# LSTM outer steps in a fused graph network: five nested outer products and two direct ones in place of four and three

## The chip, the cores and the metric

The kernel runs on one core of a Trainium2 chip. The number that counts is the device time of one execution in microseconds (us); lower is better. The engines that matter are TensorE (PE; its weight loads have a row of their own, PEld), VectorE (DVE), ScalarE (ACT) and GpSimd (POOL); loads and stores are issued by SyncE (SP). TensorE writes its products to PSUM, which has eight banks here, each wide enough for 512 fp32 columns. Everything is fp32.

## The reference, cut to what matters

Four layers are applied to x of shape (128, 64, 256), each as x = x + f(relu(layernorm(x))), with a 64 x 64 adjacency. Layer 0 is two graph convolutions and then LSTMs; layers 1 to 3 (a graph convolution with two batch norms, a three-part graph convolution, masked attention) are not touched by the change. The LSTM part of layer 0:

```python
def _lstm_last(Wih, Whh, bih, bhh, xs):
    N, _, Hd = xs.shape
    bias = bih + bhh
    def step(carry, x_t):
        h, c = carry
        g = x_t @ Wih.T + h @ Whh.T + bias
        i, f, gg, o = jnp.split(g, 4, axis=-1)
        c = jax.nn.sigmoid(f) * c + jax.nn.sigmoid(i) * jnp.tanh(gg)
        h = jax.nn.sigmoid(o) * jnp.tanh(c)
        return ((h, c), None)
    ...
for p in range(1, MAX_SKIP + 1):
    nw = Tv // p
    wins = h[:, :nw * p, :].reshape(Bv * nw, p, Hd)
    last = _lstm_last(Wih[p - 1], Whh[p - 1], bih[p - 1], bhh[p - 1], wins)
    idx = jnp.arange(nw) * p + (p - 1)
    h = h.at[:, idx, :].set(last.reshape(Bv, nw, Hd))
```

So for p = 1, 2, 3, 4 the 64 time positions are cut into windows of p successive ones, an LSTM runs p steps through each window from a zero state, and its last hidden state takes the place of the window's last position. The next p sees what the last one wrote. Hd is 256, so the four gates together have 1024 rows.

## The kernel before, in words

**Blocks and steps.** In the LSTM stage (about 340 to 1170 us of the profiled span) features lie across the 128 partitions in two chunks, and the columns are (window, batch) pairs. They are cut into blocks of N columns: 512 for p = 2 and p = 4, 352 and 320 for p = 3. Two blocks, n = 0 and n = 1, form a pair and are computed together; two pairs (the states s = 1, then s = 0) form a group, and the steps of the two alternate. A group begins with `first_step` for each pair (the step j = 0, with no h yet; matmuls at L875, reads of their banks at L884, L888 and L891), and goes on with one outer step per pair for each j = 1 to p - 1. p = 2 has two groups with two outer steps each, p = 3 two groups with four each, p = 4 one group with six: 18 outer steps. The last of them is called `fin`, and the next layer's work (the "seam") begins beside it.

**An outer step** (`outer_step`, L942) computes all gates of both blocks, G = x Wih + h Whh. It treats this as a 2 x 2 block product, (x or h) against the gate pairs (i, g) and (f, o) for the two column blocks, and computes it in the Strassen-Winograd way, with seven products of sums instead of eight: products 1 (x of block 0 with Wih of i, g), 2 (h of block 0 with Whh of i, g), 3, 4, 5, 6 and 7. The result has four parts, called by row and column "11" (i, g of block 0), "12" (i, g of block 1), "21" (f, o of block 0) and "22" (f, o of block 1), each an SBUF tile [128, 2 gates, 2 chunks, 512]. The sums of inputs are T1 = x1 - x0 (L1057, DVE), T2 = h1 - T1 (L1060, POOL), T3 = h1 - x1 (L1063, DVE) and T4 = h0 - T2 (L1066, POOL). The sums of weights (S1 to S4) and the inner sums of W1 and W2 are computed once in the graph stage on POOL, kept in DRAM (`summed`, `kept`), and loaded for each p.

**Two ways for one product.** Each outer product has two gates x 256 x 256 weights. A *direct* one (`direct`, L996 to L1007) is eight matmuls of N columns: four (gate, chunk) pairs k = 0 to 3 in the order `CHAIN`, with two contraction halves each. Pair k goes to the bank of that name, k0 to k3. Products 1, 6 and 7 are direct before, and 6 and 7 add into the banks that 1 began; after the second half of each product the bank is read (`chained`, L1013 to L1021): for 1 a copy by ACT into "11", for 6 a DVE add that makes "12" from "22" and the bank, for 7 two DVE adds, into "21" and "22". A *nested* product (`strassen`, L972 to L984) does the same kind of seven-product scheme once more on halves, in the order

```python
INNER = (("a", 1), ("c", 2), ("a", 6), ("b", 5), ("a", 7), ("b", 3), ("a", 4))
```

where each item is a bank and a half product. "5.b3" below is the item at position 3, counted from 0, of outer product 5, which is in bank b; so the items of a product are a0, c1, a2, b3, a4, b5 and a6 ("4.0" of a direct product is its first slot, "chained 7.2" the read of bank k2 after product 7). One item has two matmuls of N/2 columns, one for each gate. Products 5, 2, 4 and 3 are nested before. Bank a takes four of the items and adds them up one after the other, and is read after each; bank b takes two and is read after each; c takes one. There are two banks for a (a0, a1), used in turn by the products, and one each for b and c. The reads are `take` (L986 to L994): an ACT copy (L992) where a product is the first to write a part (items 0, 2, 3 and 6 of products 5 and 4), and otherwise a DVE add into the part (L994). The half products need sums of the halves of their inputs, four POOL subtractions of N/2 columns for each product (`inner_sum`, L967).

**What follows in a step.** When all products that belong to a part are in, ACT applies the gate functions (`act`, L1027), POOL multiplies i by g (`in_times_g`, L1037), the cell by f (`keep`, L1040), adds (`plus`, L1043), ACT takes tanh of the cell into the o-part's neighbour (`squash`, L1046), and DVE multiplies it by o (`out`, L1048): into h, or, in the last step of a window, into x. Much of this runs beside the next step's matmuls.

**What sets the order.** The kernel schedules by hand. One slot is one item of a nested product (two half-width matmuls) or one matmul of a direct one. `SEQ` (L936) spreads the 28 nested and 24 direct slots evenly over a step, 52 in all. Every operation is put into a list of events with a planned time in slots (`at`, `tick`; `prep` is a tick not earlier than the other operands' h), and the list is issued in order of time. So on each engine the order is fixed and each instruction waits only for its operands and buffers; planned times do nothing else. Loads are on SP's queue in the same list (`plan`, `load_r` L808, `fetch` L824, `fetch_s3`): while the last step of one p is computed, weights for the next are brought in. `places` (L777) tells where in SBUF each of these lie.

Of the kernel before, what the change touches and what calls it, by code (L numbers as in the profile page):

```python
# [14 lines left out]
P = 128  # L15
# [5 lines left out]
def kernel(ctx: ExitStack, tc: tile.TileContext, a: dict, out: bass.AP):  # L21
# [318 lines left out]
    SUMS = {"X": 1536, "W1": 1792, "W2": 1792, "S1": 1792, "S2": 1024, "S3": 1024, "S4": 1792}  # L340
# [8 lines left out]
    def staging(p):  # L349
# [21 lines left out]
        def kept(name, v):  # L371
            return lambda: nc.sync.dma_start(summed[p, name], v)

        def x_sum(k):
# [6 lines left out]
        work = [*(inner(W1, k) for k in (0, 1, 3)), *(inner(W2, k) for k in (0, 1, 3)),  # L381
                *(outer(add, S1_, OF_, W2, b) for b in (0, 2)), *(outer(sub, S2_, S1_, IG, b) for b in (0, 2)),
                inner(W2, 2), *(inner(S1_, k) for k in range(4)),
# [3 lines left out]
        stores = {9: ("S2", wbf[:, 5632:6656]), 10: ("W2", w2), 14: ("S1", wcf), 17: ("W1", w1),  # L387
# [389 lines left out]
    def places(p):  # L777
# [3 lines left out]
        def row(v, size):  # L781
            return chunks(v[:, :size]) if size > 0 else None

        a["W1"], a["W2"] = Blocks(2, wbf[:, 3584:5376]), Blocks(2, wbf[:, 5376:])
        a["T4"] = chunks(txf[:, : 2 * n])
        if p == 2:
            a["R"], a["X"] = Blocks(4, wbf[:, :2048]), Blocks(3, wbf[:, 2048:3584])
            a["S1"], a["S2"], a["S3o"] = Blocks(2, wcf), Blocks(2, thA[:, :1024]), Blocks(1, thA[:, 1024:])
            a["S4"] = Blocks(2, wbf[:, 2816:3328], th[:, :1280])
            a["T1"], a["T1s"], a["T2"] = chunks(waf[:, :1024]), sums(waf[:, 1024:1792], 3, h), chunks(waf[:, 1792:2816])  # L790
            a["s"], a["T3"] = sums(waf[:, 2816:], 3, h), chunks(txf[:, 1024:])
        elif p == 3:
            a["R"], a["X"] = Blocks(4, wcf[:, :1536], waf[:, :512]), Blocks(3, waf[:, 512:2048])
            a["S1"], a["S2"], a["S3o"] = Blocks(2, wbf[:, :1792]), Blocks(2, thA[:, :1024]), Blocks(1, thA[:, 1024:])
            a["S4"] = Blocks(2, th, wcf[:, 1536:])
            a["T1"], a["T1s"] = chunks(wbf[:, 1792:2496]), sums(wbf[:, 2496:3024], 3, h)
            a["T2"], a["s"], a["T3"] = (chunks(waf[:, 2048:2752]), sums(waf[:, 2752:3280], 3, h),
                                        chunks(txf[:, 1024:1728]))
        else:
            a["R"], a["X"] = Blocks(4, wbf[:, :2048]), Blocks(3, wbf[:, 2048:3584])  # L800
            a["S1"], a["S2"], a["S3o"] = Blocks(2, waf[:, 512:2304]), Blocks(2, wcf[:, :1024]), None
            a["S4"] = Blocks(2, wbf[:, 2048:3584], txf[:, 1792:])
            a["T1"] = chunks(waf[:, 2304:3328])
            a["T1s"] = [waf[:, 3328:], waf[:, :256], waf[:, 256:512]]
            a["T2"], a["T3"], a["s"] = chunks(th[:, :1024]), chunks(thA[:, :1024]), sums(wcf[:, 1024:], 3, h)
        return a

    def load_r(p):  # L808
        to, v = pl[p]["R"], weights_of("WihT", p)
        for h in range(2):  # L810
            for c in range(2):
                nc.sync.dma_start(to[2 * h + c][:, 0:2], v[h, c][:, 0:3:2])
                nc.sync.dma_start(to[2 * h + c][:, 2], v[h, c][:, 3])
        fetch_s3(p, 1)

# [8 lines left out]
    def fetch(p, name, lo=0, hi=7):  # L824
# [3 lines left out]
        hi = min(hi, v.shape[1])  # L828
# [4 lines left out]
    def input_sums(st, j):  # L833
# [4 lines left out]
        for k in range(len(t), 4):  # L838
            t.append(wide(tx[:, k, : st["N"]]))
# [14 lines left out]
    def wih_of(p, k, gi):  # L854
# [3 lines left out]
        if m < 4 and k != 7:  # L858
            return pl[p]["R"][m][:, g]
        return pl[p]["X"][(S1, S2, S3, S4).index(m)][:, g]  # L860
# [46 lines left out]
    def first_step(t0, st, tags, names):  # L907
# [20 lines left out]
        for n in range(2):  # L928
# [7 lines left out]
    SEQ = sorted([((i + 0.25) * 52 / 28, "S", i) for i in range(28)] +  # L936
                 [((k + 0.5) * 52 / 24, "D", k) for k in range(24)])
    AT = {(kind, i): n for n, (_, kind, i) in enumerate(SEQ)}
    CHAIN = ((0, 1), (1, 1), (0, 0), (1, 0))
    FN = {(0, 0): AF.Sigmoid, (0, 1): AF.Tanh, (1, 0): AF.Sigmoid, (1, 1): AF.Sigmoid}  # L940

    def outer_step(t0, st, j, tags, fin):  # L942

        N, p, blk, B = st["N"], st["p"], st["blk"], {}
        l, H, a, last = p - 1, N // 2, dict(pl[p]), j == p - 1
        if fin:
            v = gates[tags["spare"]].rearrange("p n c t -> p (n c t)")
            a["T3"], a["late"] = chunks(v[:, :1024]), sums(v[:, 1024:1792], 3, 256)
# [12 lines left out]

        def data(pr):
            v = a["T1"][:, :, :N] if pr == 5 else a["T4"][:, :, :N] if pr == 4 else h(pr == 3)
            b = {(c, d): v[:, c, d * H : (d + 1) * H] for c in range(KC) for d in range(2)}
            return b, [s[:, :H] for s in a["T1s" if pr == 5 else "late" if fin and pr != 2 else "s"]]

        def inner_sum(pr, k, engine=nc.gpsimd):  # L967
            b, s = data(pr)
            engine.tensor_sub(*((s[0], b[0, 1], b[0, 0]), (s[1], b[1, 1], s[0]),
                                (b[0, 1], b[1, 1], b[0, 1]), (s[2], b[1, 0], s[1]))[k])  # L970

        def strassen(pr, i):  # L972
# [7 lines left out]
            d = (b[0, 0], b[1, 0], b[1, 1], s[2], s[0], s[1], b[0, 1])[k - 1]  # L980
            w = a[{5: "S1", 2: "W1", 4: "W2", 3: "S4"}[pr]][OF[k]]
            for g in range(2):
                nc.tensor.matmul(B[pr, name][:, g * H : (g + 1) * H], w[:, g, :], d, start=(new and g == 0),  # L983
                                 stop=(name, k) in (("a", 4), ("b", 3), ("c", 2)), skip_group_check=True)  # L984

        def take(pr, i):  # L986
# [3 lines left out]
            to = tile_of({5: "22", 2: "11", 4: "21", 3: "12"}[pr])[:, :, hc, d * H : (d + 1) * H]  # L990
            if pr in (5, 4) and i in (0, 2, 3, 6):
                nc.scalar.copy(to, v)  # L992
            else:
                nc.vector.tensor_add(to, to, v)  # L994

        def direct(pr, k, c):  # L996
            hc, g = CHAIN[k]
            if pr == 1 and c == 0:
# [4 lines left out]
            else:  # L1003
                w = (a["R"] if pr == 1 else a["S2"])[m][:, g]
            d = x(0, c) if pr == 1 else a["T2" if pr == 6 else "T3"][:, c, :N]
            to = wide(B[k][:, :N]) if pr == 1 else B[k][:, :N]
            nc.tensor.matmul(to, w, d, start=(pr == 1 and c == 0), stop=(c == 1), skip_group_check=True)  # L1007
# [5 lines left out]
        def chained(pr, k):  # L1013
# [3 lines left out]
            elif pr == 6:  # L1017
                nc.vector.tensor_add(part("12", k), part("22", k), v)
            else:
                for m in ("21", "22"):  # L1020
                    nc.vector.tensor_add(part(m, k), part(m, k), v)  # L1021

        def act(m, g, hc):
# [3 lines left out]
            nc.scalar.activation(v, v, FN[r, g], bias=lbias[:, l, b : b + 1])  # L1027
# [20 lines left out]
        def out(n):  # L1048
            m = ("21", "22")[n]
            if last:  # L1050
                for c in range(KC):
                    (nc.gpsimd if fin and n else nc.vector).tensor_mul(x(n, c), wide(gate_(m, 0)[:, c]), wide(gate_(m, 1)[:, c]))
                return
            nc.vector.tensor_mul(h(n), gate_(m, 0), gate_(m, 1))
# [13 lines left out]
        one = j == 1 and st["s"] == 1  # L1068
# [5 lines left out]
        for c in range(KC):  # L1074
            tick(-26 + 0.6 * c if one else -30.5 + 1.6 * c, T1, c)
        for k, s in ((0, -23 if one else -28), (1, -22), (3, -21)):
            tick(s, inner_sum, 5, k)
        prep(-11, T2)
        prep(-10.9, inner_sum, 5, 2)
        for k, s in ((0, 1), (1, 2), (3, 3)):  # L1080
            prep(s, inner_sum, 2, k)
        late = 8 if one else 5
        prep(late, T4)
        prep(late + 0.1, inner_sum, 2, 2)
        late = 18 if fin else 7 if one else 1
        for c in range(KC):
            prep(late + 0.6 * c, T3, c)
        for k, s in ((0, 25), (1, 26), (3, 27), (2, 28)):
            prep(s, inner_sum, 4, k)
        for k, s in ((0, 38), (1, 38.5), (3, 39), (2, 39.5)):  # L1090
            prep(s, inner_sum, 3, k)

        for n, (_, kind, i) in enumerate(SEQ):
            if kind == "S":
                mi, i = divmod(i, 7)
                tick(n, strassen, (5, 2, 4, 3)[mi], i)
                tick(n + 1.1, take, (5, 2, 4, 3)[mi], i)
            else:
                di, i = divmod(i, 8)
                tick(n, direct, (1, 6, 7)[di], *divmod(i, 2))  # L1100
                if i % 2:
                    tick(n + 1.15, chained, (1, 6, 7)[di], i // 2)
        e = AT["S", 13] + 2.2
        for i, (g, hc) in enumerate(((0, 0), (1, 0), (0, 1), (1, 1))):
            tick(e + 0.9 * i, act, "11", g, hc)
        tick(e + 4, in_times_g, 0)
        for k, (hc, g) in enumerate(CHAIN):
            e = AT["D", 17 + 2 * k] + 2.6
            for n in range(2):
                tick(e + 0.9 * n, act, ("21", "22")[n], g, hc)  # L1110
        e = AT["D", 19] + 4.2
        for n in range(2):
            tick(e + 0.2 * n, keep, n)
        tick(e + 0.1, plus, 0)
        tick(54.6, squash, 0)
        for i, (g, hc) in enumerate(((0, 0), (1, 0), (0, 1), (1, 1))):
            tick((51.3, 53.5)[hc] + 0.1 * g if fin else (58.2, 61.2)[hc] + 1.2 * g, act, "12", g, hc)
        e = 56.2 if fin else 63
        halves = fin or last and st["s"] == 0
        for c in range(KC if halves else 1):  # L1120
            c = slice(c, c + 1) if halves else slice(0, KC)
            tick(e, in_times_g, 1, c)
            tick(e, plus, 1, c)
        tick(61 if fin else 58.5, out, 0)
        squashed, done = (6.5, 8.8) if last and p < NL else (5, 8) if N < 512 else (4.2, 6)
        tick(e + squashed, squash, 1)
        tick(e + done, out, 1)
        st["h_at"] = t0 + e + done
        return t0 + 52
# [4 lines left out]
    def plan(t, p, *when):  # L1134
        for s, fn, *args in when:
# [3 lines left out]
    plan(t, 2, (2, load_r), *((8 + 3 * k, fetch, name) for k, name in enumerate(("X", "W1", "W2", "S1", "S2"))),  # L1139
         (25, fetch, "S4", 2, 7), (28, fetch_s3, 0))  # L1140
    for p in range(1, NL + 1):
        pairs = pairs_of(p)
        for k in range(0, len(pairs), 2):
# [15 lines left out]
            if p == 2:  # L1159
                plan(t, p, (8, fetch, "S4", 0, 2))  # L1160
# [845 lines left out]
```

## Time and profile before

| | |
|---|---|
| median of 3 runs | 1822.1 us |
| lowest and highest | 1821.66 and 1826.21 us |
| the profiled execution's own time | 1826.36 us |
| its span | 1824.6 us |
| granted TensorE clock | 0.999 of full speed |
| PE busy in the span | 1800.3 us |
| DVE, ACT, POOL busy | 1179.4, 988.5, 1205.9 us |
| PE at L983 (nested) and L1007 (direct), share of the chain that ended last | 20% and 17% |

The rows of busy time are of one profiled execution. Matmuls overlap their neighbours, so PE's busy time can cover small gaps. A row of a group of instructions names line, engine, operation, the tile written and the tiles read, the count, busy time and mean of one, and then the idle time of the engine ahead of them with what ended it. In a timeline, the columns are the start in us from the start of the span, the duration, the engine, the line and operation, the tiles, the shape and the number of instructions joined in one row; what stands in brackets at a row's end is the engine's idle time ahead of it and what released it.

### The profile page before, as it was taken

To read this page: it belongs to the slowest core of one execution; us is meant where nothing else is said; L and a number is where in the kernel's file an instruction comes from. 1 tells how busy PE (TensorE), PEld (TensorE's weight loads), DVE (VectorE), ACT (ScalarE), POOL (GpSimd) and SP (SyncE) were. 2 spreads that over 40 slices of the span, in tenths; PEclk is the share of its full clock that TensorE was granted. 3 is DMA by queue.
4 is the path that set the end of the run, shared out by engine and by line. 5 is a ranking of instruction groups with operands and counts; after the bars stand their busy time and mean duration, and the time that the engine had idled before them with its cause. 6 is when DMAs were issued, how large, how long until landed. Compare 5 with 4: busy or idle time off the path is not lost.

```text
span 1824.6 us, 24389 instructions
## 1 busy us (share of the span) xinstructions
PE 1800.3 (99%) x8532; PEld 1299.8 (71%) x8532; DVE 1179.4 (65%) x2346; ACT 988.5 (54%) x1773; POOL 1205.9 (66%) x1215
## 2 busy tenths in 40 slices
PE   8999999999999999999999999999999999999998
PEld 7988444466566887787466666656444899999997
DVE  6875545565566666666556666788876566666664
ACT  6766666644645545544634444687674454444442
POOL 7988454766676777777677776776363666666663
PEclk9999999999999999999999999999999999999999
DMA  6854300000003000003000000433200010111111
GB/s 182 260 169 159 129 0 0 7 1 9 6 24 116 1 1 1 1 1 113 26 0 1 1 1 5 140 125 121 61 1 16 32 47 22 38 47 47 47 47 35
DMA packets 67786, 93.04 MB, mean 51 GB/s; under 512 B 4816, under 2 KB 57808, under 8 KB 67664
## 3 DMA queue, kind: packets, MB, share of 16 engines
q1 hardware_dynamic: 67216, 91.19, 15.0%
q8 instruction: 68, 1.11, 0.3%
q14 instruction: 54, 0.44, 0.1%
q10 hardware_dynamic: 448, 0.30, 0.1%
HBM read 56.99 MB, written 34.47 MB: 50 GB/s over the span
## 4 chain that ended last, share of the span: by engine, by line
PE 92%; POOL 3%; DVE 2%; ACT 2%; issue 2%; DMA 0%; POOLq 0%; DVEq 0%; ACTq 0%
PE ps L983 20%; PE ps L1007 17%; PE ps L875 15%; PE ps L1730 8%; PE ps L1212 5%; PE ps L1457 4%; PE ps L1817 3%; PE ps L463 3%; PE ps L453 3%; PE ps L1697 3%; PE ps L1793 2%; PE ps L492 2%; PE ps L1827 2%; PE ps L1858 1%; PE ps L722 1%
## 5 line engine op out<-in xcount | busy, mean ns | idle before, releaser
L994 DVE TENSOR_TENSOR gate<-gate,ps 128x512 f32<-128x512 f32 (+2 forms) x360 | 216.3, 602 | 184.9 <-PE ps L983 174.0
L1027 ACT ACTIVATE gate<-gate,lbias 128x512 f32<-128x512 f32 (+2 forms) x288 | 175.6, 652 | 171.2 <-DVE gate L994 86.8
L888 DVE TENSOR_TENSOR gate<-gate,ps 128x512 f32<-128x512 f32 (+2 forms) x162 | 100.7, 640 | 129.2 <-PE ps L875 118.9
L992 ACT COPY gate<-ps 128x512 f32<-128x512 f32 (+2 forms) x144 | 74.9, 520 | 155.6 <-PE ps L983 155.1
L875 PE MATMUL ps<-tx,wih 128*128 128x512 f32 (+2 forms) x276 | 117.8, 544 | 1.9 <-ACT gate L891 1.4
L1673 ACT ACTIVATE h<-x,ln_rn 128x256 f32<-128x256 f32 x128 | 68.0, 592 | 92.8 <-POOL ln_rn L1670 92.7
L884 ACT ACTIVATE gate<-gate,lbias 128x512 f32<-128x512 f32 (+2 forms) x108 | 95.8, 887 | 29.1 <-DVE gate L888 29.0
L1730 PE MATMUL ps<-wl,ag 128*128 128x128 f32 x900 | 108.3, 276 | 0.6
L1730 PEld LDWEIGHTS ps<-wl,ag 128*128 128x128 f32 x900 | 104.2, 192 | 3.3 <-ACT ag L1702 2.5
L1037 POOL TENSOR_TENSOR gate<-gate 128x1024 f32<-128x1024 f32 (+4 forms) x41 | 73.8, 1800 | 42.1 <-ACT gate L1027 42.1
L983 PEld LDWEIGHTS ps<-h,wb 128*128 128x128 f32 x392 | 71.1, 190 | 39.6 <-issue 22.0
L1021 DVE TENSOR_TENSOR gate<-gate,ps 128x512 f32<-128x512 f32 (+2 forms) x144 | 80.7, 602 | 22.3 <-PE ps L1007 20.2
L983 PE MATMUL ps<-h,wb 128*128 128x256 f32 (+2 forms) x392 | 91.3, 355 | 0.0
L875 PEld LDWEIGHTS ps<-tx,wih 128*128 128x128 f32 x276 | 51.5, 190 | 55.6 <-issue 39.5
L891 ACT COPY gate<-ps 128x512 f32<-128x512 f32 (+2 forms) x108 | 59.4, 550 | 53.1 <-PE ps L875 52.5
L840 POOL TENSOR_TENSOR tx<-hT 128x512 f32<-128x512 f32 (+2 forms) x29 | 36.0, 1242 | 75.8 <-PE ps L875 73.8
L1040 POOL TENSOR_TENSOR cell<-cell,gate 128x1024 f32<-128x1024 f32 (+2 forms) x36 | 73.0, 2029 | 19.1 <-ACT gate L1027 19.1
L922 POOL TENSOR_TENSOR cell<-gate 128x1024 f32<-128x1024 f32 (+2 forms) x36 | 78.1, 2192 | 5.4 <-ACT gate L884 5.4
L1007 PE MATMUL ps<-hT,wb 128*128 128x512 f32 x160 | 81.7, 592 | 0.0
L1007 PE MATMUL ps<-wih,thA 128*128 128x512 f32 (+2 forms) x192 | 79.3, 495 | 0.0
L875 PE MATMUL ps<-hT,wih 128*128 128x512 f32 (+2 forms) x168 | 78.5, 572 | 0.4 <-DVE h L499 0.4
L1043 POOL TENSOR_TENSOR cell<-cell,gate 128x1024 f32<-128x1024 f32 (+4 forms) x41 | 74.1, 1808 | 3.2
(338 smaller groups left out, 4960.3 us busy)
## 6 DMA issues: line engine op xcount, KB each, us to landing
xt<-in_x_dram SPq DMA_DIRECT2D x30, 512.0 KB, 4.5
x1d<-xt SPq DMA_DIRECT2D x16, 512.0 KB, 2.9
x<-x1d SPq DMA_DIRECT2D x16, 512.0 KB, 4.8
out_dram<-x SPq DMA_DIRECT2D x15, 512.0 KB, 3.4
W<-wb SPq DMA_DIRECT2D x6, 896.0 KB, 4.6
wb<-W SPq DMA_DIRECT2D x6, 896.0 KB, 5.2
wb<-in_WihT_dram SPq DMA_DIRECT2D x32, 128.0 KB, 3.8
wb<-in_WhhT_dram SPq DMA_DIRECT2D x24, 128.0 KB, 3.9
```

Source lines behind the costliest of these rows:

```text
L875: nc.tensor.matmul(wide(p_[:, :N]), wih_of(p, k, gi), x_, start=first_, stop=True, skip_group_check=True)
L884: nc.scalar.activation(to, r[bank_][:, :N] if bank_ else to, fn, bias=lbias[:, l, m : m + 1])
L888: nc.vector.tensor_add(slot(n, hc), slot(n, hc), r[bank_][:, :N])
L922: nc.gpsimd.tensor_mul(cell[:, n, :, :N], i, g_)
L983: nc.tensor.matmul(B[pr, name][:, g * H : (g + 1) * H], w[:, g, :], d, start=(new and g == 0), stop=(name, k) in (("a", 4), ("b", 3), ("c" ...
L992: nc.scalar.copy(to, v)
L994: nc.vector.tensor_add(to, to, v)
L1007: nc.tensor.matmul(to, w, d, start=(pr == 1 and c == 0), stop=(c == 1), skip_group_check=True)
L1021: nc.vector.tensor_add(part(m, k), part(m, k), v)
L1027: nc.scalar.activation(v, v, FN[r, g], bias=lbias[:, l, b : b + 1])
L1212: nc.tensor.matmul(r[name], con["w1"][:, OF[j], g, :], x_, start=new, stop=(name, j) in (("a", 4), ("b", 3), ("c", 2)), skip_group_check=True)
L1730: nc.tensor.matmul(v["g", name][:, p_, :], x_[:, m, ts(p_, P)], wl2[:, OF[j], m, :], start=new and p_ == m == 0, stop=m == 2 and (name, j) ...
```

## The change

The seven outer products are divided in another way. Products 1, 6, 5, 3 and 2 are nested, in this order, 35 slots; only 7 and 4 are direct, 16 slots, so that a step has 51. Product 4 adds into the banks that 7 began. A bank k0 to k3 is read after 7's second half, by one DVE add that makes "22" from "12" and the bank, and again after 4's, by one DVE add into "21". Parts are built in other orders: product 1 is taken into "11" by ACT copies (items 0, 2, 3, 6) and DVE adds; 6 into "21" on top of "11", and 5 into "12" on top of "21", so their first takes are DVE adds of two different tiles (`BASE`) instead of copies; 3 adds to "12" and 2 to "11". Per step there are thus 39 DVE reads of PSUM and 4 ACT copies, where there were 32 and 12.

The order of slots comes from `order_of`, in three versions: `SEQ`, `FIRST` for the first outer step of a group's first pair (`one`: j = 1, s = 1), in which product 7 begins later, and `LAST` for `fin`, in which 5, 2 and 3 are nested and 1, 6, 7 and 4 direct (53 slots). Product 1's inner sums are four new POOL subtractions per step on x of block 0; their results lie in the tile "22" until that part is written.

The four parts of the cell work have new places in the step: "12" and "22" (block 1) are finished first, and "11" and "21" (block 0) at the step's end, so that `act` "11", `in_times_g` 0, `plus` 0, `squash` and `out` 0 run beside the next step's first products. `out` is issued in two halves by chunk.

The weights follow: S2 now gets inner sums (stored in 2048 columns, from `s2_sum`), W2 is loaded without its inner sums straight from Whh (`fetch_w2`), X holds what product 1 needs (inner sums S1, S2, S4 of Wih for i and g, with S3's stored in R), `fetch_fin` brings the two blocks that `fin` needs otherwise, and the loads for the next p stand later in the plan: `load_r` at 31.5 slots instead of 12.5, W1 at 51.5 instead of 25.5, W2 at 52 instead of 38.5.

```diff
-    SUMS = {"X": 1536, "W1": 1792, "W2": 1792, "S1": 1792, "S2": 1024, "S3": 1024, "S4": 1792}
+    SUMS = {"X": 1536, "W1": 1792, "S1": 1792, "S2": 2048, "S3": 1024, "S4": 1792}
...
-        work = [*(inner(W1, k) for k in (0, 1, 3)), *(inner(W2, k) for k in (0, 1, 3)),
+        work = [*(inner(W1, k) for k in (0, 1, 3)),
...
-                inner(W2, 2), *(inner(S1_, k) for k in range(4)),
+                *(s2_sum(k) for k in range(4)), *(inner(S1_, k) for k in range(4)),
...
-    SEQ = sorted([((i + 0.25) * 52 / 28, "S", i) for i in range(28)] +
-                 [((k + 0.5) * 52 / 24, "D", k) for k in range(24)])
...
+    def order_of(*rows):
+        v = [(t0 + step * k, name, k) for name, n, t0, step in rows for k in range(n)]
+        return [e[1:] for e in sorted(v)]
+
+    SEQ, FIRST = (order_of(*((pr, 7, (i * 7 + 0.25) * 51 / 35, 51 / 35) for i, pr in enumerate((1, 6, 5, 3, 2))),
+                           (7, 8, t, step), (4, 8, 32, 2.3)) for t, step in ((2.5, 3.2), (9, 2.5)))
+    LAST = order_of((5, 7, 0, 1.7), (2, 7, 13, 2.8), (3, 7, 33, 2.8),
+                    (1, 8, 0.5, 1.5), (6, 8, 12.6, 1.5), (7, 8, 25, 1.6), (4, 8, 38.5, 1.6))
...
+        direct_ = (1, 6, 7, 4) if fin else (7, 4)
+        one = j == 1 and st["s"] == 1
+        seq = LAST if fin else FIRST if one else SEQ
+        place = {v: n for n, v in enumerate(seq)}
+        DEST = {5: "22", 2: "11", 3: "12"} if fin else {1: "11", 6: "21", 5: "12", 3: "12", 2: "11"}
+        BASE = {} if fin else {6: "11", 5: "21"}
...
-            to = tile_of({5: "22", 2: "11", 4: "21", 3: "12"}[pr])[:, :, hc, d * H : (d + 1) * H]
-            if pr in (5, 4) and i in (0, 2, 3, 6):
+            to, new = tile_of(DEST[pr])[:, :, hc, d * H : (d + 1) * H], i in (0, 2, 3, 6)
+            if new and pr == seq[0][0]:
                 nc.scalar.copy(to, v)
             else:
-                nc.vector.tensor_add(to, to, v)
+                base = tile_of(BASE[pr])[:, :, hc, d * H : (d + 1) * H] if new and pr in BASE else to
+                nc.vector.tensor_add(to, base, v)
...
-            elif pr == 6:
-                nc.vector.tensor_add(part("12", k), part("22", k), v)
+            elif fin:
+                nc.vector.tensor_add(part("12" if pr == 6 else "22", k), part("22", k), v)
             else:
-                for m in ("21", "22"):
-                    nc.vector.tensor_add(part(m, k), part(m, k), v)
+                nc.vector.tensor_add(part("22" if pr == 7 else "21", k), part("12" if pr == 7 else "21", k), v)
...
+        if not fin:
+            for k in range(4):
+                tick(-6.6 + 0.8 * k if one else -26 + 0.1 * k, inner_sum, 1, k)
...
+            if i % 2 and not (fin and pr == 4):
+                after = max(n, place[5, 5 + k % 2]) if pr == (6 if fin else 7) else n
+                read[pr, k] = after + 1.15 + (0 if fin or pr == 4 else (0, 1.0, 1.2, 3.0)[k])
+                tick(read[pr, k], chained, pr, k)
...
+            tick(done[2] + 0.9 * i if fin else (52.4, 52.7, 55.3, 56.3)[i], act, "11", g, hc)
...
+        soon = last and (st["s"] == 0 or p == NL)
+        tick(36, keep, 1)
+        tick(45.1, in_times_g, 1)
+        tick(45.2, plus, 1)
+        tick(53.5, squash, 1)
+        e = 57 if soon else 60
+        tick(50.5 if soon else e, keep, 0)
+        tick(e + 0.1, in_times_g, 0)
+        tick(e + 0.2, plus, 0)
+        e += 5.5 if soon else 9.5
+        tick(e, squash, 0)
+        for c in range(KC):
+            tick(55.5 + 1.5 * c, out, 1, c)
+            tick(e + 1.3 + 0.8 * c, out, 0, c)
+        st["h_at"] = t0 + e + 2.1
+        return t0 + len(seq)
...
-                plan(u, q, (12.5, load_r), (36, fetch, "X"), (25.5, fetch, "W1"), (38.5, fetch, "W2"),
+                plan(u, q, (31.5, load_r), (36, fetch_x), (51.5, fetch, "W1"), (52, fetch_w2),
                      (52.5, fetch, "S1"), (53.5, fetch, "S2"))
```

## The prediction

> **What bounds it now.** I read the page's engine line first, then the stretches of the LSTM stage, then the timeline of single slots. The page:
>
> ```profile
> PE 1800.3 (99%) x8532; PEld 1299.8 (71%) x8532; DVE 1179.4 (65%) x2346; ACT 988.5 (54%) x1773; POOL 1205.9 (66%) x1215
> PE 92%; POOL 3%; DVE 2%; ACT 2%; issue 2%; DMA 0%; POOLq 0%; DVEq 0%; ACTq 0%
> ```
>
> PE is busy nearly always and carries 92% of the chain that ended last. The stretches (columns: us, then busy us and count of PE, PEld, DVE, ACT, POOL) say the same of outer steps, the first of p = 2, the second of p = 3:
>
> ```profile
> 353.00:448.00 95.00, 95.00 (x334) 63.20 (x333) 57.21 (x80) 39.26 (x61) 61.11 (x47) 1.00 0.02 8
> 596.00:720.00 124.00, 124.00 (x661) 103.86 (x659) 79.96 (x158) 58.86 (x123) 89.01 (x96) 1.00 0.00 1
> ```
>
> So a slot taken off PE is worth its full length, as long as no other engine makes PE wait. What a slot costs, and how soon its bank is read, is in the timeline. For N = 512:
>
> ```profile
> 1001.63 1.03 PE L983 MATMUL ps<-h,wb 128*128 128x256 f32 x4
> 1002.50 1.02 PE L1007 MATMUL ps<-hT,wb 128*128 128x512 f32 x2
> 1002.70 0.69 DVE L994 TENSOR_TENSOR gate<-gate,ps 128x512 f32<-128x512 f32 x1 [0.93 <-PE ps L983]
> 1003.36 1.03 PE L983 MATMUL ps<-wc,wb 128*128 128x256 f32 x4
> ```
>
> and for N = 352, with two nested slots in a row:
>
> ```profile
> 701.22 0.76 PE L983 MATMUL ps<-h,wb 128*128 128x176 f32 x4
> 701.82 0.76 PE L983 MATMUL ps<-wih,wb 128*128 128x176 f32 x4
> 702.02 1.12 DVE L994 TENSOR_TENSOR gate<-gate,ps 128x352 f32<-128x352 f32 x2 [0.67 <-PE ps L983]
> 702.42 0.75 PE L1007 MATMUL ps<-wih,thA 128*128 128x352 f32 x2
> ```
>
> Starts count here, not durations. A nested slot (two half products, four passes) takes 0.863 us, a direct one 0.858; for N = 352 both 0.594; for N = 320 the same view gives 0.55 and 0.54. An idle DVE starts its read 1.07 us after the slot's start (1002.70 - 1001.63), 0.80 for N = 352, 0.755 for 320. One read takes 0.683, 0.518 and 0.484 us in the groups kept apart by shape. The last thing wanted is what a wait of PE on such a read costs. There is one, at the seam:
>
> ```profile
> 1170.84 1.27 DVE L994 TENSOR_TENSOR gate<-gate,ps 128x512 f32<-128x512 f32 x2
> 1171.57 0.73 PEld L983 LDWEIGHTS ps<-gate,wb 128*128 128x128 f32 x4 [0.95 <-DVE gate L994]
> 1171.57 1.13 PE L983 MATMUL ps<-gate,wb 128*128 128x256 f32 x4 [0.76 <-DVE gate L994]
> 1172.54 0.59 PE L1007 MATMUL ps<-gate,wb 128*128 128x512 f32 x1
> ```
>
> The first of the two reads ends at about 1171.50; PE goes on 0.07 later and then needs 0.97 us for a slot of 0.86, as its weight load was not ahead of it. So a read that PE waits for costs its end + 0.18 us.
>
> [...] the busy 1.03 us of a 0.86 us slot agrees, so 100% busy hides waits up to 0.17 us and I count starts. [...] the trace has 683 and 518. Reads do not shrink with N as slots do. [...] here a 1024-column POOL sum beside such Vector work took 3.39 us, else 2.36.
>
> **The change, part by part.** The steps with one slot less: 17 (nine of N = 512, four of 352, four of 320). N = 512: 28 x 0.863 + 24 x 0.858 = 44.76 becomes 35 x 0.863 + 16 x 0.858 = 43.93, -0.83, nine times -7.4. N = 352: -0.59, four times -2.4. N = 320: 28 x 0.55 + 24 x 0.54 = 28.36 to 27.89, four times -1.9. The last step (LAST) has 21 nested and 32 direct, 53 slots: 45.58, +0.8. Sum on PE: -10.9 us. Weight loads rise from 160 to 172 a step; two nested slots in a row keep 0.594 for N = 352 (four loads in it), so loads do not bind.
>
> What is read from PSUM moves. Before, a step had 28 nested and 16 direct reads, 12 of them ACT copies and 32 DVE adds; after, 35 + 8, 4 on ACT and 39 on DVE. DVE gets 7 x 0.683 = 4.8 us a step, about 33 of 43.9 us with T1, T3 and the outputs: not full, so hidden by PE on average. But bank a is read after each of its four products and b after its first, before PE may add the next. Before, these pairs lay 4, 4, 3 and (b) 4 slots apart; in SEQ they lie 3 apart, and in product 5 both 5.a4 to 5.a6 and 5.b3 to 5.b5 only 2, because order 5.b3 5.a4 5.b5 5.a6 3.a0 has no direct slot. I work that stretch by hand, us from 5.b3, N = 512 (read-after-write on DVE adds 0.05):
> read 5.b3 1.07 to 1.755, so 5.b5 goes at 1.935 for 1.72: +0.21. Read 5.a4 1.93 to 2.62, 5.a6 at 2.80 just in time. Read 5.b5 3.01 to 3.69; then chained 7.0 to 4.43; it frees the bank that direct 4.0 wants at 4.52, and gets at 4.60: +0.09. Read 5.a6 to 5.07, chained 7.2 to 5.71, read 3.a0 5.76 to 6.44, so 3.a2 goes at 6.62 for 6.32: +0.30. Together 0.60 us.
> The same with 0.80 / 0.518 / 0.594 gives 0.31 + 0.29 + 0.33 = 0.93 for N = 352, and 0.98 for 320. In FIRST one direct slot lies between: 0.22 + 0.16 = 0.38 for 512, 0.65 for 320.
>
> ACT loses 8 copies a step but its four sit at the step's start, among acts of the step before: take 1.a0, two act "11", squash 1, take 1.a2, act, take 1.b3. N = 512 (act 0.65 back to back, squash 1.04): 1.b3 is out at 5.80, 1.b5 is due at 6.03: nothing. N = 352 (0.52, 0.75, copy 0.43): 1.a2 out at 3.47, 1.a4 due at 3.56 goes at 3.65, and 1.b5 due at 4.25 at 4.60: 0.44; for 320, 0.56. Only steps after another outer step have this. Outputs of the step before stand in DVE's queue ahead of read 5.a0: 0.08 to 0.24 for p = 3, about 0.15 for p = 2, nothing for p = 4.
>
> Sum of waits: p = 2: 2 x 0.38 + 2 x 0.75 = 2.3. p = 3: 2 x 0.65 + 4 x 352-steps (twice 1.45, twice 1.61) + 2 x 1.62 = 10.7. p = 4: 0.38 + 4 x 0.60 = 2.8. Together 15.7 us.
>
> POOL gets four input sums (N/2 columns, 0.73 us) a step, 2.9 of 43.9; it stands behind nothing that PE wants soon, except where noted below. Stored sums: four sums for four in the graph stage. The loads of the next p move later (31.5 instead of 12.5 for R): eight issues at about half a microsecond and about 4 us to landing end some 3 us before the next p's first slot for N = 352; SP has nothing else queued there. Late by a whole landing, twice, costs 8 us at most; I take 0. The summed S4 needs no second X load. ACT copies at the end and the tail's order: 0, PE has seam work there.
>
> **Sum.** -10.9 + 15.7 = +4.8 us. The profiled execution took 1826.36 us round a span of 1824.6 and so is 4 us above the median 1822.1; differences within it are put on the median: 1827.
>
> **Rivals.** A, the slots come through. If Vector reads in a queue start closer than I put them (pairs at L1021 lie 0.64 apart, not 0.68) and ACT is in time, only the two-slot pairs stay: 6 x 0.21 + 4 x 0.31 + 2 x 0.33 + 3 x 0.22 + 2 x 0.33 = 4.5 us. -10.9 + 4.5 = -6.4, 1816; without those 1811. It ends faster; it decides once the waits at 3.a2, at direct 4.0 and at ACT together stay under 1 us a step of p = 3. For it: DVE is at 65%; against it: its work is bunched just there, and five nested slots give PE 0.594 each against 0.518 a read plus two chained adds.
>
> B, a new wait on POOL. take 1.a0 writes the tile that plus 1 of the step before reads. keep 1, four sums, T2, in-times-g and plus 1 stand in one queue: for N = 512 plus 1 ends 0.85 us before take 1.a0 could start, for 352 about 0.1. If T2 is slowed as above (+1.0 us, 0.7 for 352) and plus 1 too, each of 12 steps starts its ACT reads 0.5 to 1 us late, and PE waits at 1.a4 and 1.b5: about +7, 1834. It decides where both POOL operations meet T1 and T3 on DVE, which their places allow.
>
> C, the loads bind after all or the step isn't shorter, as each nested slot has twice the instructions: +0.01 us a slot for 320 gives 2 us, 1829. The starts above speak against it.
>
> **Chances.** Forecast 0.50 (1821 to 1834), A 0.27 (1810 to 1820), B 0.18 (1831 to 1841), C 0.05. Eight in ten: from A's middle to B's upper part, 1813 to 1838. A measurement tells about 0.3%, 5.5 us: faster below 1816.6, slower above 1827.6. A below that line gives 0.24; of the forecast 0.29 and the rest of A and C fall within, 0.34; the rest, 0.42, is slower.
>
> **What would show it.** PE rows: 616 nested and 304 direct slots. Right: PE waiting for the line of take (DVE) some 25 times or more, at the second half of product 5 and at 3.a2, 0.1 to 0.4 us each, more in the p = 3 stretch; PE waiting for ACT copies at 1.b5 there; p = 3 stretches longer than before (30.9 us for an N = 352 step), p = 4 ones shorter by about 0.2. Wrong: p = 3 steps at 30.3 us (A), or ACT's copies waiting for POOL's plus (B), or first steps of a p waiting for a DMA.

## The result, and the profile after

The changed kernel takes 1829.72 us (median of 6, 1828.75 to 1834.7) where the kernel before takes 1821.88 beside it: a ratio of 1.0041, 95% interval 1.0029 to 1.0053. Run again in the experiments below, it was 1830.13 beside 1826.17, a ratio of 1.0027 (1.0017 to 1.0037). So it is slower, by 4 to 8 us. The changed kernel's median hardly moved between the two; that of the kernel before did, because its executions fall into groups near 1822, 1825, 1826.5 and 1828 us. In the first comparison four of six lay in the lowest group, beside all the experiments only four of 101. No run shows what makes that group.

The page of the changed kernel, engine line and chain:

```profile
PE 1804.0 (98%) x8724; PEld 1323.7 (72%) x8724; DVE 1245.3 (68%) x2474; ACT 927.1 (51%) x1633; POOL 1248.9 (68%) x1271
PE 54%; DVE 2%; ACT 1%; POOL 1%; issue 1%; DMA 0%; SPq 0%; DVEq 0%; POOLq 0%; ACTq 0%
```

DVE has 66 us more, ACT 61 us less; that is mostly the copies that became adds. PE is busy 3.7 us longer although it has 16 slots less: its busy time covers most of its waits. The chain's shares sum to only about 60% of the span, so this row tells only that PE leads it. The two stretches that answer to those shown of before (us, then busy us and count of PE, PEld, DVE, ACT, POOL):

```profile
354.00:449.00 95.00, 94.73 (x359) 67.18 (x358) 66.48 (x96) 32.92 (x48) 67.94 (x55) 1.00 0.00 1
601.00:725.00 124.00, 122.61 (x698) 105.56 (x697) 92.19 (x186) 46.95 (x91) 94.48 (x108) 1.00 0.00 1
```

DVE went from 60% to 70% of p = 2's steps and from 64% to 74% of p = 3's; nowhere is it full.

Where PE stands can be read from its starts, as in the prediction. From the first start of a step to the next matmul after it, in us; the last two columns are experiments that are told below:

| step | before | after | product 5 not read | last version |
|---|---|---|---|---|
| N = 512, SEQ (6) | 44.77 | 44.50 | 43.95 | 44.24 |
| N = 352, SEQ (4) | 30.91 | 31.25 | 30.35 | 31.11 |
| N = 320, SEQ (2) | 28.39 | 29.17 | 28.00 | 28.95 |
| N = 512, FIRST (3) | 47.35 | 47.4 | 47.1 | 46.65 |
| N = 320, FIRST (2) | 30.05 | 31.62, 31.77 | 31.0, 31.1 | 30.4, 30.6 |
| N = 512, LAST (1) | 50.36 | 50.67 | 50.67 | 50.67 |
| sum of 18 steps | 701.55 | 706.62 | 695.08 | 699.40 |
| between p = 2 and p = 3 | 25.01 | 26.95 | 26.95 | 26.04 |
| between the groups of p = 3 | 22.75 | 23.30 | 23.29 | 23.10 |
| between p = 3 and p = 4 | 35.13 | 33.62 | 33.62 | 33.62 |

(A FIRST step has slots of the other pair's first step in it.) Where their code is the same, the steps repeat to 0.04 us in every profile, except the FIRST steps of N = 320, which come out 0.15 apart; so elsewhere differences of 0.05 us a step can be read. The profiled execution after had a span of 1833.0, 8.4 us more than that of before: 5.1 in the steps, 1.1 between them, 1.25 in the graph stage ahead of the LSTM, 1.0 behind it. A second profile of the same kernel began its first outer step 4.7 us earlier, at 351.87 us, so the difference in the graph stage is no more than its own scatter. Of the 1.0 us behind the LSTM about 0.6 comes with the change: in every profile of a changed kernel the next layer's matmuls run that much later than in the one of before, from the place where they join the last step.

**The waits of a step.** The changed kernel's timeline in a step of p = 4 (start, duration, engine, line, tiles); 5.b5 starts at 975.44 and 3.a0 at 977.34:

```profile
976.20 1.30 PE L1036 MATMUL ps<-wih 128*128 128x256 f32 x5
...
976.61 0.69 DVE L1048 TENSOR_TENSOR gate<-gate,ps 128x512 f32<-128x512 f32 x1 [0.36 <-PE ps L1036]
...
977.34 0.69 DVE L1076 TENSOR_TENSOR gate<-gate,ps 128x512 f32<-128x512 f32 x1
977.34 1.03 PE L1036 MATMUL ps<-h,wb 128*128 128x256 f32 x4
977.94 0.68 DVE L1048 TENSOR_TENSOR gate<-gate,ps 128x512 f32<-128x512 f32 x1
...
978.54 0.68 DVE L1076 TENSOR_TENSOR gate<-gate,ps 128x512 f32<-128x512 f32 x1
...
979.32 0.69 DVE L1048 TENSOR_TENSOR gate<-gate,ps 128x512 f32<-128x512 f32 x1
...
980.16 0.67 PE L1036 MATMUL ps<-wc,tx 128*128 128x256 f32 x2
```

These are, on DVE, the reads of 5.b5, chained 7.0, 5.a6, chained 7.2 and 3.a0. They follow one another nearly without a gap; the last ends at 980.01, and 3.a2 goes at 980.16 where its slot was due at 979.92. The five DVE reads are what the prediction worked out by hand (3.a0 read from 5.76 to 6.44 us after 5.b3; here it is 5.68 to 6.37). The view of waits gives PE just six waits for L1048, 2.2 us in all, because a row of matmuls stands as busy beyond the next slot's start: 3.a0 has 1.03 us from 977.34, and the next slot starts at 978.20, 0.86 later, so a wait of up to 0.17 us does not show. Against the undisturbed spacing of the starts, PE is late at the second half of product 5 and again at 3.a2 in each of the 17 steps, more often than the 25 times that the prediction named, and the time lost is more than five times 2.2 us.

**The first step of a group** has a wait that was not foreseen, between 7.3 and 6.b5 (N = 320, changed kernel, timeline):

```profile
610.55 2.01 DVE L884 TENSOR_TENSOR h<-gate 128x704 f32<-128x704 f32 x2
...
611.57 0.70 PE L1063 MATMUL ps<-tx,wih 128*128 128x320 f32 x2
...
612.49 1.07 DVE L1048 TENSOR_TENSOR gate<-gate,ps 128x320 f32<-128x320 f32 x2
...
613.02 0.81 PE L1036 MATMUL ps<-wih,wb 128*128 128x160 f32 x4 [0.74 <-DVE gate L1048]
```

6.b3 could have been read at 611.24 (its slot's start, 610.49, + 0.755). The two products for h of the other pair's first step (`state`, L884) stand ahead of that read in DVE's queue; it starts at 612.49, and PE is 0.91 us late. For N = 512 the same place costs 0.36.

### The profile page after: what moved, and what is told of

It is laid out like the page before. It is cut to its first block, busy times and chain, and to the rows that moved or that the text cites. A ratio compares the mean times of both kernels' runs of the same rounds, so it can differ in the third digit from the quotient of the medians.

```text
span 1833.0 us, 24875 instructions
## 1 busy us (share of the span) xinstructions
PE 1804.0 (98%) x8724; PEld 1323.7 (72%) x8724; DVE 1245.3 (68%) x2474; ACT 927.1 (51%) x1633; POOL 1248.9 (68%) x1271
## 4 chain that ended last, share of the span: by engine, by line
PE 54%; DVE 2%; ACT 1%; POOL 1%; issue 1%; DMA 0%; SPq 0%; DVEq 0%; POOLq 0%; ACTq 0%
PE ps L1036 13%; PE ps L1797 8%; PE ps L1063 7%; PE ps L1279 5%; PE ps L1524 4%; PE ps L1884 3%; PE ps L1764 3%; PE ps L1860 2%; PE ps L908 2%; PE ps L1894 2%; PE ps L1925 1%; PE ps L736 1%; PE ps L1832 1%; PE ps L1708 1%; PE ps L689 1%
## 5 line engine op out<-in xcount | busy, mean ns | idle before, releaser
L1048 DVE TENSOR_TENSOR gate<-gate,ps 128x512 f32<-128x512 f32 (+2 forms) x544 | 326.4, 601 | 171.7 <-PE ps L1036 155.4
L921 DVE TENSOR_TENSOR gate<-gate,ps 128x512 f32<-128x512 f32 (+2 forms) x162 | 100.4, 641 | 127.3 <-PE ps L908 119.3
L1063 PE MATMUL ps<-tx,wb 128*128 128x512 f32 (+2 forms) x320 | 145.1, 535 | 0.0
L908 PE MATMUL ps<-tx,wih 128*128 128x512 f32 (+2 forms) x252 | 110.7, 555 | 0.1
L924 ACT COPY gate<-ps 128x512 f32<-128x512 f32 (+2 forms) x108 | 59.4, 551 | 55.7 <-PE ps L908 54.8
L1076 DVE TENSOR_TENSOR gate<-gate,ps 128x512 f32<-128x512 f32 (+2 forms) x136 | 81.1, 596 | 5.1 <-PE ps L1063 3.4
L1093 POOL TENSOR_TENSOR gate<-gate 128x1024 f32<-128x1024 f32 (+3 forms) x37 | 73.9, 1997 | 9.3 <-ACT gate L1082 9.0
L1036 PEld LDWEIGHTS ps<-h,wb 128*128 128x128 f32 x328 | 58.8, 190 | 23.4 <-issue 11.7
L1099 POOL TENSOR_TENSOR cell<-cell,gate 128x1024 f32<-128x1024 f32 (+3 forms) x37 | 73.6, 1989 | 2.9
L1036 PE MATMUL ps<-h,wb 128*128 128x256 f32 (+2 forms) x328 | 74.9, 351 | 0.0
L1021 POOL TENSOR_TENSOR wih<-wih 128x256 f32<-128x256 f32 (+2 forms) x88 | 65.9, 760 | 8.4 <-DVE wih L1114 5.5
L908 PE MATMUL ps<-tx,wb 128*128 128x512 f32 x144 | 68.7, 594 | 0.0
```

The source lines that it names most:

```text
L908: nc.tensor.matmul(wide(p_[:, :N]), wih_of(p, k, gi), x_, start=first_, stop=True, skip_group_check=True)
L921: nc.vector.tensor_add(slot(n, hc), slot(n, hc), r[bank_][:, :N])
L1036: nc.tensor.matmul(halves_of(to) if pr == 1 else to, w, d, start=(new and g == 0), stop=(name, k) in (("a", 4), ("b", 3), ("c", 2)), skip_ ...
L1048: nc.vector.tensor_add(to, base, v)
L1063: nc.tensor.matmul(to, w, d, start=new, stop=(c == 1), skip_group_check=True)
L1076: nc.vector.tensor_add(part("22" if pr == 7 else "21", k), part("12" if pr == 7 else "21", k), v)
```

## The experiments

Each is compared with the kernel before, run beside it on the same chip (1826.2; 1825.9 in the last pair). The first four ran on one chip, so that the changed kernel's 1830.13 was measured beside them. The run without the reads and the first two put together ran on a second chip, the last pair on a third, and the changed kernel was not run there: for these a difference from 1830.13 is one between chips, and the steps of the profiles are the better measure.

**The changed kernel again.**

> The changed kernel as it is, beside the runs below. It should again be about 7.5 us slower than the kernel before (1829.5 where that takes 1822). In its profile the 17 outer steps and the last one should repeat to 0.05 us each (44.50 for N = 512, 31.25 for 352, 29.17 for 320, 47.4 and 31.7 for the first of a group), since these come from fixed waits. What does not repeat, such as the 1.3 us by which the graph stage before the LSTM was longer, or the 1.0 us after it, is not of the change.

1830.13 us (1829.71 to 1830.99), 1.0027 of before (1.0017 to 1.0037): slower again, though by 4 us and not 7.5, since the kernel before was slower here. The steps repeat: 44.50, 31.25, 29.17, a sum of 706.65. The stretch from p = 2 to p = 3 is 26.95 again.

**The order of slots.** In SEQ and FIRST:

```diff
-    SEQ, FIRST = (order_of(...) for t, step in ((2.5, 3.2), (9, 2.5)))
+    SEQ, FIRST = ([(int(v[0]), int(v[1])) for v in w.split()] for w in (
+        "... 64 65 66 50 75 51 52 76 53 54 77 55 56 30 40 31 41 32 33 42 34 35 43 36 20 44 21 22 45 ...",
+        "... 65 74 66 50 75 51 52 76 53 54 77 55 56 30 40 31 41 32 33 42 34 35 43 36 20 44 21 22 45 ..."))
```

> Only the order of slots: in product 5 the direct slots stand so that no two items of one bank are nearer than three slots, in product 6 one pair (6.a4 to 6.a6) is now two apart, and both 4.0 and 4.1 stand between 3.a0 and 3.a2. If PE waits because reads by DVE come late (the forecast's reason), the 0.25 us at 5.b5 to 3.a0 and the 0.31 at 3.a2 go for N = 512 (0.38 and 0.37 for p = 3) and 0.2 to 0.3 come at 6.a6: a step of N = 512 takes 44.15 instead of 44.50, of 352 about 30.75 instead of 31.25, and the whole is 4 to 5 us shorter than the changed kernel, about 1825. If nested slots cost more in themselves (their weight loads, or five products' worth of instructions), the order changes nothing: 1829.5.

1830.34 us, no change where 1825 was expected. By steps it is two results. For N = 512 the waits at 5.b5, 5.a6 and 3.a2 are gone, 0.25 comes at 6.a6 (the pair now two apart), and a step takes 44.24 to 44.27: as expected, a little less of it. For N = 352 a step takes 31.4 to 31.6 and for 320 29.76, longer than with the old order. There the same waits are gone and others have come, at 5.a2 (0.22 and 0.42) and at 2.a2 (0.14 and 0.33). DVE at 5.a2, N = 352, in this kernel:

```profile
639.72 0.52 DVE L1051 TENSOR_TENSOR gate<-gate,ps 128x352 f32<-128x352 f32 x1 [0.49 <-PE ps L1039]
640.16 0.71 DVE L1114 TENSOR_TENSOR h<-gate 128x320 f32<-128x320 f32 x1
640.79 0.51 DVE L1051 TENSOR_TENSOR gate<-gate,ps 128x352 f32<-128x352 f32 x1
```

L1051 are the reads of 6.a6 and 5.a0 here, L1114 the output of the step before; it took its place between them because 6.b5, 6.a6 and 5.a0 now come in a row. At 2.a2 the same is done by T1. So the wait follows the order of DVE's queue, and spacing alone does not remove it where DVE has other work in the way.

**The two h products of a first step.** For the second pair of a group:

```diff
-            at(h_at + 0.8 * n, state, st, n, g["o"], g["g"], p == 1)
+            at(h_at + 0.8 * n if p == 1 or st["s"] else t + (16.2, 18.2)[n], state, st, n, g["o"], g["g"], p == 1)
```

> Only two DVE instructions per group are moved: the first step's two products for h of the second pair (each 0.88 to 1.22 us) stood ahead of the read of 6.b3 and are put behind the reads of 6.a4 and of 6.b5. If they are what PE waits for between 7.3 and 6.b5 in the first outer step of a group, that wait (0.46 us for N = 512, 1.0 for N = 320) goes in five groups: 3 x 0.46 + 2 x 1.0 = 3.4 us shorter than the changed kernel, about 1826. If PE waits there only for the spacing of bank b's items (three slots, as elsewhere without a wait), or for the inner sums of product 6 on POOL, nothing changes: 1829.5.

1826.33 us, 1.0004 of before (0.9996 to 1.0013), 3.8 less than the changed kernel. The wait at 6.b5 is gone in all five groups: FIRST takes 46.95 for N = 512 and 30.75 for N = 320, and the steps sum to 703.34, 3.31 less (expected 3.4). N = 320's FIRST had 31.63 and 31.76, so 0.9 to 1.0 us each. In the timeline of this kernel the reads of 6.b3 and 6.a4 now stand ahead:

```profile
605.25 1.08 DVE L1048 TENSOR_TENSOR gate<-gate,ps 128x320 f32<-128x320 f32 x2 [0.59 <-PE ps L1036]
...
606.13 0.71 PE L1036 MATMUL ps<-wih,wb 128*128 128x160 f32 x4
606.25 0.92 DVE L884 TENSOR_TENSOR h<-gate 128x704 f32<-128x704 f32 x1
```

**The last tanh of a group.**

```diff
-        e += 5.5 if soon else 9.5
+        e += 9.8 if soon and p < NL and st["end"] == (p == 2) else 5.5 if soon else 9.5
```

(`end` is true in the last group of a p.)

> Only one ACT instruction is moved, in two places: the last tanh of a group (squash 0), from p = 2 to p = 3 and between the groups of p = 3, is put some four slots later, behind the copies of the next first step. If PE waits in those first steps because ACT stands at this tanh until POOL's sum of the cell is ready, the 1.9 us there and about 0.5 between the groups go: 2 to 2.5 us shorter than the changed kernel, about 1827. If PE waits for loads of p = 3's weights, which the change put later, or the delay is made up by waits that follow anyway (a part was, in the trace: 5.1 us late at its worst, 3.0 some 10 us on), it stays within 0.5 us of 1829.5.

1831.04 us: a miss, and a little more than even the second reading of the expectation allows (within 0.5 us of 1829.5). From p = 2 to p = 3 the wait of 1.90 us is gone, but 0.30 and 1.30 us of waits for ACT follow, and the stretch takes 25.43 us, while other kernels that keep the 1.90 us take 25.3 to 25.9 there where nothing else is added (see below). Between the groups of p = 3 it is 1.1 us longer than unmoved, 24.40. So the delay ends at a later wait whatever stands first, which was the second reading of the expectation.

What the stretch does cost was told by comparing profiles. The changed kernel's second profile, and then that of the run with the h products moved, at the same place (us, busy us of the engines, and the granted clock, the third number from the end):

```profile
577.40:580.80 3.40, 1.50 (x6) 0.87 (x5) 1.47 (x3) 2.56 (x5) 0.81 (x1) 1.00 0.99 337
580.80:584.20 3.40, 3.40 (x8) 2.12 (x7) 2.57 (x6) 1.78 (x4) 1.91 (x2) 0.50 0.80 295
```

```profile
577.40:580.80 3.40, 1.49 (x6) 0.77 (x5) 1.22 (x3) 2.31 (x4) 1.06 (x1) 1.00 1.01 349
580.80:584.20 3.40, 3.40 (x14) 2.31 (x13) 2.83 (x7) 2.03 (x5) 2.70 (x4) 1.00 0.82 300
```

Both waited 1.9 us for ACT; in the first, 3.4 us at half clock follow, 8 matmul passes instead of 14, and 1.7 us are lost. The half clock is there in four of the eight profiles of changed kernels in which PE waits in one piece, and in neither of the two in which it does not.

**Product 5 not read.** The DVE reads of product 5 are left out where 7 and 4 alone are direct:

```diff
-                tick(n + 1.1, take, pr, i)
+                if fin or pr != 5:
+                    tick(n + 1.1, take, pr, i)
```

> The seven DVE reads of product 5 are left out in the 17 steps where it is nested beside 7 and 4, so the gates lack product 5; PE's work and its order are unchanged. If PE's waits from 5.b5 to 3.a2 come from DVE's queue (reads of product 5, then two reads of product 7 ahead of the read of 3.a0), all of them go: a step of N = 512 takes 43.95 instead of 44.50, of 352 30.3 instead of 31.25, of 320 28.3 instead of 29.17; 11 us less than the changed kernel, about 1819. If the slots themselves or the weight loads of five nested products cost, the steps stay; if only the two-slot pairs count and the wait at 3.a2 has another cause (product 3's inner sums on POOL), 0.25 to 0.38 a step goes, 5 us in all: 1825.

1818.95 us, 11.2 less than the changed kernel on the other chip (expected 11), 0.9957 of before (0.9945 to 0.9970). The steps sum to 11.5 us less. A step of N = 512 takes 43.95, of 352 30.35, of 320 28.00; SEQ has no waits left except those for ACT at 1.b5 for N = 320. In its timeline the slots from product 5 to 3.c1 follow one another as planned, 0.86 us each:

```profile
963.85 1.03 PE L1036 MATMUL ps<-h,wb 128*128 128x256 f32 x4
...
964.71 1.02 PE L1063 MATMUL ps<-tx,wb 128*128 128x512 f32 x2
...
964.97 0.69 DVE L1048 TENSOR_TENSOR gate<-gate,ps 128x512 f32<-128x512 f32 x1 [6.19 <-PE ps L1036]
...
965.57 0.59 PE L1036 MATMUL ps<-h,ready 128*128 128x256 f32 x2
```

So five nested products cost no more than their slots, weight loads included, and all of the wait from 5.b5 to 3.a2 goes when the reads of product 5 are gone from DVE's queue.

**Put together.** The new order for N = 512; for p = 3 the old order up to product 5 with a new end; the h products moved. Then two edits on ACT's order; then the last tanh of p = 2 as well. Of the code, the order of slots for p = 3, and ACT's order in the last version:

```diff
+        "10 11 70 12 13 71 14 15 72 16 60 61 73 62 63 74 64 65 75 66 50 76 51 52 77 "
+        "53 54 55 56 30 40 31 41 32 33 42 34 35 43 36 20 44 21 45 22 23 46 24 25 47 26",
...
-            tick(done[2] + 0.9 * i if fin else (52.4, 52.7, 55.3, 56.3)[i], act, "11", g, hc)
+            tick(done[2] + 0.9 * i if fin else (52.4, 52.7, *((56.15, 57) if N == 352 and not last else (55.3, 56.3)))[i], act, "11", g, hc)
...
-        e += 5.5 if soon else 9.5
+        e += 9.8 if p == 2 and soon and st["end"] else 7.1 if soon and p == 3 and not st["end"] else 5.5 if soon else 9.5
```

> Put together from what helped: the moved h products of the first step; the new order of slots for N = 512 alone (it gave 0.26 to 0.33 a step there and lost as much at p = 3); for p = 3 the order of the changed kernel up to product 5, and then 4.0 and 4.1 both between 3.a0 and 3.a2, with two direct slots kept between 2.a0 and 2.a2. By the reads theory the steps sum to 706.65 - 3.3 - 2.5 - 0.8 = 700.0 us, 1.5 less than before (701.55), and the whole is about 7 us shorter than the changed kernel, 1823, level with the kernel before or a little under it. If the gains do not add (DVE has a bound of its own in these steps), the sum stays at 702 or above.

1823.32 us, 0.9986 of before (0.9979 to 0.9992). The steps sum to 699.81 (expected 700.0): the gains add.

> As the last, and on ACT two things moved: the third and fourth act 11 of the first N = 352 step of a p = 3 pair behind the copy of 1.b3 in the next step (there PE waited 0.35 us at 1.b5, twice), and the last tanh between the groups of p = 3 behind one copy of the next first step (there PE waited 0.43). If both waits are ACT's order, 0.7 + 0.4 us go: 1.1 us less than the last run, with 28.7 instead of 29.0 in the two later N = 320 steps. If acts that come later only move the wait (to the sums of the cell on POOL and so to T4), these steps stay as they are.

1822.88 us, 0.9984 (0.9977 to 0.9991); steps 699.46. Of the 1.1 us expected from the two edits, 0.4 came. In the later N = 320 steps the wait at 1.b5 fell from 0.35 to 0.10, but that at 5.a2, behind the outputs of the step before, rose from 0.20 to 0.35: 28.95, where 28.7 was expected and the run before had 29.07. The outputs come when they come, and PE only reached them sooner. Its profile has the half clock between p = 2 and p = 3 (27.57 us).

> As mix2, with the last tanh from p = 2 to p = 3 also put later, as in the run that moved it alone. There the 1.9 us wait in one piece went and shorter waits came (0.30 and 1.30), so the stretch between the two p was 25.4 us; where the wait stays in one piece it was 25.3 to 25.9 without, and 27.0 to 27.6 with 3.4 us of half clock behind it (in four of seven profiled executions). If the half clock follows from the idle time in one piece, this kernel's profile has none there and 25.5 to 26 us, and the median is 0.5 to 1 us below mix2's 1822.9. If the half clock comes from something else, it will be there again in about every second execution and the median stays.

1822.54 us, 0.9985 (0.9978 to 0.9992), beside the same kernel without the last edit:

> mix2 again, beside the last on the same chip. The steps should repeat to 0.05 us, with a sum of 699.5; the stretch from p = 2 to p = 3 is 25.9 or 27.6 us as half clock falls on it or not.

1823.61 us, 0.9987 (0.9980 to 0.9994), steps 699.52, the stretch 25.90, with no half clock this time. The last version has none either and takes 26.04. One profile of it cannot settle the cause, and a median 1.1 us lower, with both ranges over 3 us wide, is no more than in keeping with it. Its page:

```profile
PE 1796.7 (99%) x8724; PEld 1323.0 (73%) x8724; DVE 1241.7 (68%) x2474; ACT 923.7 (51%) x1633; POOL 1249.3 (69%) x1271
```

So the change with a part of its waits taken away is about 0.15% faster than the kernel before was beside it, not 11 us, as the slots alone would have it. Its median does not pass the group near 1822 us in which four of the first six executions of the kernel before lay.

## Why the prediction was right, and where not

The forecast was 1827 (1813 to 1838), slower by 5; it came to 1829.7, slower by 7.8. The sum over the steps was forecast at +4.8 us and is +5.07, but this closeness is luck, made of errors of both signs: 4.4 us too little for FIRST, against 2.7 too much for the waits of p = 3, 0.4 for those of p = 2 and 0.5 for LAST. What was right is the mechanism and the size of its main term.

- **PE's saving** (-0.83, -0.59, -0.47 a step): shown. Without the reads of product 5, the N = 512 step is 0.82 under before and the 352 one 0.56. For 320 it is 0.39, with 0.35 us of ACT's wait in the step after and 0.23 of waits in the one before: 0.51 without them.
- **The stretch of product 5** (0.60, 0.93, 0.98 in SEQ; 0.38 and 0.65 in FIRST): shown to 0.08 us. Against the run without these reads it is 0.55 and 0.90 for N = 512 and 352; for 320, whose total difference is 1.17, the starts of the two runs from 5.b3 on give 0.96. In FIRST they give 0.33 to 0.37 and 0.65. Of the parts, the 0.09 at 4.0 is not there for N = 512; the slot of 5.a6 is 0.07 longer instead. This term alone is 11 us, as much as the whole saving.
- **ACT at 1.b5** (0, 0.44, 0.56): wrong for 352, where PE does not wait at all; for 320 the wait is there, but with 0.35 us (1.b5 was due at 667.78):

```profile
667.57 0.42 ACT L1045 COPY gate<-ps 128x320 f32<-128x320 f32 x1
...
668.04 0.81 PE L1036 MATMUL ps<-hT,wih 128*128 128x160 f32 x4
```

- **Outputs ahead of the read of 5.a0** (0.08 to 0.24 for p = 3, 0.15 for p = 2): only N = 320 has it, 0.20 at 5.a2. With ACT's this made the forecast of the 352 steps too long by 0.5 to 0.7 each, and that of the waits of p = 3 by 2.7 us.
- **FIRST** was the step of the sum that failed: it was forecast 0.45 shorter than before for N = 512 and 0.18 longer for N = 320, and it is up to 0.09 and 1.6 to 1.7 longer, 4.4 us in five groups. The step "outputs of the step before stand in DVE's queue" was worked for outer steps and not for the first step of the other pair, whose h products stand in that queue at 6.b3. Moving them gave 3.3 us back. The rest, 0.5 us a group for N = 320, is at 1.c1 and 1.a6 (0.55 to 0.7 us by the starts) and was not tested.
- **LAST** (+0.8): +0.31.
- **Loads and the seams** (0): the loads cause no wait that a run shows. Between p = 2 and 3 and between the groups of p = 3 there is 2.5 us more, 1.7 of it the half clock, which only part of the executions have; between p = 3 and 4 there is 1.5 us less, because a copy by ACT and an input sum by POOL, for which PE stood before, come in time now (in the kernel before, 888.23 was due at 887.55):

```profile
886.69 1.02 PE L875 MATMUL ps<-hT,wb 128*128 128x512 f32 x2
888.23 1.13 PE L875 MATMUL ps<-tx,wb 128*128 128x512 f32 x2 [0.51 <-ACT gate L891]
889.63 1.13 PE L875 MATMUL ps<-tx,wb 128*128 128x512 f32 x2 [0.27 <-POOL tx L840]
```

Behind the LSTM there is 0.6 more.

Rival A (1816) was right that reads in a queue start closer than the forecast put them. Its mark was set badly: it was to decide once the waits at 3.a2, at 4.0 and at ACT together stay under 1 us a step of p = 3. They do, with about 0.5 us for 352 and 0.9 for 320, and still A did not come, as its sum took them for nothing and lacked FIRST's wait. Its step of 30.3 us was seen only where the reads are left out. Rival B took its slowed sum from the kernel before, where T4 takes 3.39 us from 992.83, beside DVE's output from 992.80 (1.21 us). It has nothing in the trace after for it: no copy of product 1 waits for POOL's sum of the cell, and for N = 512 neither T2 (2.35 to 2.40 us) nor that sum (2.36 at most) is longer than before. Rival C is excluded by the run without the reads, where each nested slot takes 0.86 us.

## What to carry to other kernels

Work taken off the engine that bounds a kernel is worth its length only if the reads of its results keep up where they come thickest. Here DVE was 70 to 74% busy on average, and a stretch where ten reads fall in a row gave back 11 us, as much as was saved. Work such a stretch out instruction by instruction, in the order of the reading engine's queue, with everything else in that queue, also from other steps; what was left out of that list is what went wrong here. And a wait that is removed can be given to the next one in the queue, as the last tanh and the wait at 1.b5 show: look for what is late next before moving it.

## What was not expected of the hardware

- TensorE fell to half clock behind an idle piece of 1.9 us, in four of the eight profiled executions that have it. In the changed kernel PE goes on at 584.35 after 1.90 us; the granted clock is 1.00 to 584.66, 0.50 for the 3.41 us to 588.07, and then 1.00 again. In the run with the h products moved PE goes on at 579.91 after 1.91 us, and the clock stays at 1.00. So the length of this piece alone does not decide; what does was not shown.
- DVE reads of PSUM that stand ready in its queue can start 0.60 us apart for 512 columns (977.34, 977.94 and 978.54 in the changed kernel) and 0.43 for 352 (652.62 and 653.05 in the run with the new order), closer than the 0.69 and 0.52 us that each lasts; the reads before and after those three stand 0.73 and 0.78 away. The prediction took 0.68 for most of them, and so its hand-worked waits were a little long.
- After such a wait PE's slot itself was 0.10 us longer in nearly every case (0.07 to 0.12; at 3.a2 the next slot starts at 981.09, 0.93 after 980.16 where 0.86 is usual); the prediction's 0.11, from one place in the kernel before (0.97 for 0.86), held.
